# Spectral layer's way back for two blocks at a time, and seven products for all gates of one-node LSTMs

## The chip, the cores and the metric

The kernel runs on one core of a Trainium2 chip. Its time is the device time of one execution in microseconds, as the median over runs. A core has TensorE (PE, with weight loads listed apart as PEld), VectorE (DVE), ScalarE (ACT), GpSimd (POOL) and SyncE (SP), which issues most DMAs. Each runs its own queue of instructions in order; semaphores tie them together.

## What is computed

The input x has 128 batch entries of 64 nodes with 256 features, in float32. Four layers with skip connections follow each other, each on h = relu(layernorm(x)). Layer 0 is a graph convolution with batch norms, layer 3 an attention over 512 edges. The change touches layers 1 and 2:

```python
# layer 1 (U: eigenvectors of the graph's Laplacian, 64 x 64)
agg = jnp.einsum('mn,bnd->bmd', U.T, features)
h = jax.nn.relu(agg @ W1 + b1)
out = h @ W2 + b2
return jnp.einsum('nm,bmd->bnd', U, out)            # the way back

# layer 2: two graph convolutions, then LSTMs over windows of p nodes
for p in range(1, MAX_SKIP + 1):                     # 1 to 4
    nw = Tv // p
    wins = h[:, :nw * p, :].reshape(Bv * nw, p, Hd)
    last = _lstm_last(Wih[p - 1], Whh[p - 1], bih[p - 1], bhh[p - 1], wins)
    idx = jnp.arange(nw) * p + (p - 1)
    h = h.at[:, idx, :].set(last.reshape(Bv, nw, Hd))

# one step of the LSTM; state and cell start at zero
i, f, gg, o = jnp.split(x_t @ Wih.T + h @ Whh.T + bias, 4, axis=-1)
c = sigmoid(f) * c + sigmoid(i) * tanh(gg)
h = sigmoid(o) * tanh(c)
```

For p = 1 a window is a single node: there is no earlier state, the forget gate drops out, and h = sigmoid(o) * tanh(sigmoid(i) * tanh(gg)) overwrites each node.

## The kernel before

**Layout.** The 128 x 64 rows are cut into NB = 16 blocks of 8 batch entries. `X0` to `X15` are SBUF tiles of 128 partitions x 1024 floats that hold x, block by block. While layer 2's LSTMs run, x is spilled to DRAM and the X tiles serve as scratch; the nodes' features lie transposed in `big`, four groups of 32 batch entries (`nodes(q)`), each with two halves of 256 features on 128 partitions.

**Layer 1** (`layer1`, line 2030) is software-pipelined in an order written out by hand. Round i does `first(i)` (W1 and relu: "ps<-a,w"), `back(i - 1)` (the way back: eight 64x64-tiled matmuls "ps<-y,BDUT", then two adds onto X[i - 1]), `mixed(i + 1)` (agg: "ps<-BDU,h"), `second(i)` (W2 and bias: "pt<-w,g", then two adds into y), `end0(i + 3)` (layer 0's last transposes: "pe") and the layer norm of block i + 2. PSUM has four banks "ps", two "pt" and two "pe". Within a round a scheduler may move instructions between engines' queues by its own estimate of durations; `nc.hold(marks)` ties each instruction of a round to come after the previous round's last one on its engine.

**The LSTMs** (`windows`, line 2268) go through p = 1 to 4. The nodes of one p are cut into chunks of up to 16 windows x 16 + 16 batch entries; chunks are done two at a time. A step of one chunk (`lstm`, line 2358) first writes differences of its inputs into a tile T ("ls_tx<-big", a subtraction of 512 and two of 256 columns). Then `gates` computes two gates at once by Strassen's scheme in Winograd's form: seven products of halves of the weights and of the batch in place of eight. One product is two matmuls of 256 columns, one for each gate. Weight sums (`weights`, "ls_s", or sums in X tiles) stand ready; sums of products run through Z and U on DVE; sigmoids and tanhs run on ACT, in place in a tile V of "ls_g":

```python
a = product(1, "a", True)
self.act(Z, a, AF.Copy)
o.add(Z, Z, product(6, "b", True))
o.add(U, Z, product(7, "f", True))
o.add(V[:, :, 1, 1], U, product(5, "d", True))
a = product(2, "a", False)          # then activations of V[:, :, 0, 0] from PSUM
o.add(V[:, :, 1, 0], Z, product(4, "f", False))
o.add(V[:, :, 0, 1], Z, product(3, "d", False))
```

"f" and "d" are PSUM banks used twice: product 4 adds onto what product 7 left there, product 3 onto product 5, and so each has to wait until DVE has read the first sum.

For p = 1 a chunk needs three gates: input and candidate together by the seven products, and the output gate alone, by four direct matmuls of 512 columns (the branch `if p == 1 and len(xs) == 1`). The cell's product (128x1024), and the last state (`last_state`, two halves of 512), are multiplied on DVE. There are 4 groups x 4 = 16 chunks, so eight pairs.

**Order.** `nc.ordered` is off here: the same scheduler arranges each engine's instructions by its estimates, and dependences and the reuse of buffers bound it. `weights(p)` loads p's weights by DMA when the second pair of chunks of p - 1 begins. For p = 1 and 3 they lie in X tiles (X4 to X7 for the input weights, X0 to X3 for the recurrent ones), for p = 2 and 4 in tiles of their own. As the differences, weight sums and Z and U sums share DVE's queue, one that waits holds up those behind it.

Of the kernel before, what the change touches and what calls it, by code (L numbers as in the profile page):

```python
# [8 lines left out]
F32 = mybir.dt.float32  # L9
I32 = mybir.dt.int32  # L10
AF = mybir.ActivationFunctionType
ALU = mybir.AluOpType
# [901 lines left out]
class Fast:  # L914
# [28 lines left out]
    def act(self, out, a, f, **kw):  # L943
        return self.nc.scalar.activation(out, a, f, **kw)
# [499 lines left out]
B, N, D = 128, 64, 256  # L1444
P = 128
NB = 16
TPB = 4
BT = 512
# [18 lines left out]
class Kernel:  # L1467
# [35 lines left out]
    def begin(self):  # L1503
        nc, o, io = self.nc, self.o, self.io
        self.ident = self.c("ident", P, P)
        make_identity(nc, self.ident)
        self.ones = self.c("ones", P, P)
        nc.vector.memset(self.ones[:], 1.0)
        self.A, self.AT = self.c("A", N, N), self.c("AT", N, N)
        nc.sync.dma_start(self.A[:], io["adj"])  # L1510
        nc.sync.dma_start(self.AT[:], io["adj_t"])
        self.X = []
        for i in range(NB):
            self.X.append(self.c(f"X{i}", P, TPB, D))
        self.load_x(0)

    def load_x(self, i):
# [512 lines left out]
    def layer1(self, pool, psum, ps2, ps0, tables, after):  # L2030
        nc, o = self.nc, self.o
        (W1, W2), b1, b2 = self.W1, self.b1, self.b2
        nc.fresh()
        nc.ordered = True
        p = psum.tile([P, BT], F32, name="ps")
        self.warm(p[:, 0:P], 8)
        hs, as_, gs, ys = {}, {}, {}, {}

        def mixed(i):
            a = as_[i] = pool.tile([P, 2, BT], F32, name="a")  # L2040
            self.mix(psum, hs.pop(i), self.BDU, lambda dc, p: self.act_copy(a[:, dc, :], p[:]), True)

        def first(i):
            p = psum.tile([P, BT], F32, name="ps")
            a = as_.pop(i)
            for kc in range(2):
                self.mm(p[:], W1[:, kc, :], a[:, kc, :], kc == 0, kc == 1)
            g = gs[i] = pool.tile([P, BT], F32, name="g")
            self.act(g[:], p[:], AF.Relu, bias=b1[:, 0:1])

        def second(i):

            g = gs.pop(i)
            y = ys[i] = pool.tile([P, 2, 2, D], F32, name="y")
            for k in range(2):
                p = ps2.tile([P, 2, D], F32, name="pt")
                for c in range(2):
                    self.mm(p[:, c, :], g[:, (2 * k + c) * P:(2 * k + c + 1) * P], W2[:, 0, :])
                o.add(y[:, k, :, :], p[:], b2[:, None, :].to_broadcast([P, 2, D]))

        def back(i):

            y = ys.pop(i)
            ps = [psum.tile([P, 2, D], F32, name="ps") for r in range(2)]
            for c in range(2):
                for r in range(2):
                    s = slice(64 * r, 64 * r + 64)
                    self.mm(ps[r][64 * c:64 * c + 64], self.BDUT[s, s], y[s, :, c, :])
            for r in range(2):
                x = self.X[i][:].rearrange("p (k r) d -> p r k d", r=2)[:, r]  # L2070
                o.add(x, x, ps[r][:])


        self.features1(0)
        self.features1(1)
        self.residual(ps0, 0, (0, 2))
        by = self.moments(pool, 0)
        self.residual(ps0, 1, (0,))
        by = self.factors(pool, *by)
        self.residual(ps0, 1, (2,))  # L2080
        p = psum.tile([P, BT], F32, name="ps")
        self.warm(p[:, 0:P], 10)
        hs[0] = self.norm(pool, 0, by=by)
        by = self.moments(pool, 1)
        mixed(0)
        by = self.factors(pool, *by)
        hs[1] = self.norm(pool, 1, by=by)
        self.features1(2)
        marks = nc.mark()
        for i in range(NB + 1):  # L2090
            if i < NB:
                first(i)
            if i == 4:
                tables()
            if i:
                back(i - 1)
            if i + 1 < NB:
                mixed(i + 1)
            if i < NB:
                second(i)  # L2100
            if not i:
                self.residual(ps0, 2, (0, 2))
            if i + 3 < NB:
                self.end0(i + 3, ps0)
            if i + 2 < NB:
                hs[i + 2] = self.norm(pool, i + 2)

            nc.ordered = False
            nc.hold(marks)
            marks = nc.mark()  # L2110
            if i == NB - 1:
                nc.hold()
                after()
# [154 lines left out]
    def windows(self):  # L2268
# [4 lines left out]
        nc, o, io = self.nc, self.o, self.io  # L2273
        cx, (w, wq, gp, tp, zp, psum, pst) = self.stage([("lsw", 1), ("lswq", 1), ("lsg", 2), ("lst", 2), ("lsz", 2),
                                                         ("lsps", 7), ("lstps", 1)], "tile")
        with cx:
# [3 lines left out]
                nc.sync.dma_start(bias[:], io["L2_gnn_bih"].rearrange("q (k p) -> p q k", p=P))  # L2280
                nc.sync.dma_start(bh[:], io["L2_gnn_bhh"].rearrange("q (k p) -> p q k", p=P))
            o.add(bias[:], bias[:], bh[:])
            flat = [x[:].rearrange("p t d -> p (t d)") for x in self.X]
            self.c_, self.h_, self.th_ = Ring(flat[12:15]), Ring(flat[8:10]), Ring(flat[10:12])
            self.u_ = Ring([flat[15][:, 0:512], flat[15][:, 512:1024]])
            self.lp = gp, tp, zp, psum, bias
# [9 lines left out]
            def weights(p):  # L2296

                out = []
                for n, m in enumerate(("Wih", "Whh") if p > 1 else ("Wih",)):
                    t = load(None, n, None if p % 2 == 0 else 4 - 4 * n)  # L2300
                    ap = io[f"L2_gnn_{m}_t"][p - 1]
                    for kc in range(2):
                        nc.sync.dma_start(t[kc], ap[kc * P:(kc + 1) * P, :])
                    A = [[t[kc].rearrange("p (x k m) -> p x k m", k=2, m=P)[:, :, k, :] for kc in range(2)]
                         for k in range(2)]
                    S1, S2, S4 = (y.rearrange("p (x m) -> p x m", m=P) for y in t[2:5])
                    o.add(S1, A[1][0], A[1][1])
                    o.sub(S2, S1, A[0][0])
                    o.sub(S4, A[0][1], S2)
                    S3 = t[5].rearrange("p (x m) -> p x m", m=P) if len(t) > 5 else A[1][0]  # L2310
                    o.sub(S3, A[0][0], A[1][0])
                    out.append({1: A[0][0], 2: A[0][1], 3: S4, 4: A[1][1], 5: S1, 6: S2, 7: S3,
                                "A": A})
                return out

            ready = weights(1)
            for p in range(1, 5):
                Ws = ready
                nw = N // p
                parts = -(-nw // 16)  # L2320
                chunks = []
                for q in range(NG):
                    w0 = 0
                    for k in range(parts):
                        w1 = w0 + (nw - w0) // (parts - k)
                        chunks.append((q, w0, w1))
                        w0 = w1
                for n in range(0, len(chunks), 2):
                    if n == 2 and p < 4:
                        ready = weights(p + 1)  # L2330
                    if n == 2 and p == 4:
                        self.fetch(0, 8)
                        for i in range(8):
                            self.back(i, pst, "pt")
                    two = [dict(q=q, w0=w0, w1=w1) for q, w0, w1 in chunks[n:n + 2]]
                    two[-1]["last"] = p == 4 and n + 2 >= len(chunks)
                    for t in range(p):
                        for ch in two:
                            self.lstm(p, t, ch, Ws)
# [18 lines left out]
    def lstm(self, p, t, ch, Ws):  # L2358
# [25 lines left out]

        def gates(xs, fs):
            G = gp.tile([P, 2, 1024], F32, name="ls_g")
            if p == 1 and len(xs) == 1:
                for k in range(2):
                    ps = psum.tile([P, BT], F32, name="ps")
                    for kc in range(2):  # L2390
                        self.mm(ps[:, 0:2 * W].rearrange("p (w b) -> p w b", b=32), Ws[0]["A"][k][kc][:, xs[0], :],
                                node(kc), kc == 0, kc == 1)
                    self.act(G[:, 0, 2 * W * k:2 * W * (k + 1)].rearrange("p (h w b) -> p h w b", h=2, b=16),
                             ps[:, 0:2 * W].rearrange("p (w h b) -> p h w b", h=2, b=16), fs[0],
                             bias=bias[:, p - 1, 2 * xs[0] + k:2 * xs[0] + k + 1])
                return G
            n = len(xs)
            V = G[:, 0:n, 0:4 * W].rearrange("p x (k h w) -> p x k h w", k=2, h=2)
            banks = {}
# [57 lines left out]
        else:  # L2457
            self.last_state(H, at, W, s(G, 0), s(G, 1))

    def last_state(self, H, at, W, *factors):  # L2460

        for k in range(2):
            y = H[:, k, at, :].rearrange("p w (h b) -> p h w b", h=2)
            self.o.mul(y, *(x[:, 2 * W * k:2 * W * (k + 1)].rearrange("p (h w b) -> p h w b", h=2, b=16) for x in factors))

# [470 lines left out]
```

## Time and profile before

| | us |
|---|---|
| median of three runs | 2251.39 (2249.25 to 2252.05) |
| profiled execution | 2249.32 |
| its span | 2247.5 |
| PE busy | 2207.4 (98%) |
| DVE busy | 1629.2 (72%) |
| ACT busy | 1153.4 (51%) |
| POOL busy | 37.9 (2%) |
| LSTMs over single nodes, 672.19 to 825.34 | 153.15 |

The granted TensorE clock is 0.997 of full speed. Nearly all instructions are recorded at one helper's line, L800, so the profile's groups are told apart by engine, operation and tiles: "ps<-ls_tx,X" is a matmul into a PSUM tile ps, with ls_tx and X as its operands, and "x12" a run of twelve records. A matmul of full float32 leaves two records. Times are in us unless marked ns; a row's first number in the timeline is its start from the span's beginning, the second its duration up to the last record's end. In a group's row the numbers after the bar are the busy time, the mean of one in ns, and the idle time ahead of them with what ended it.

### The profile page before, as it was taken

To read this page: it belongs to the slowest core of one execution; us is meant where nothing else is said; L and a number is where in the kernel's file an instruction comes from. 1 tells how busy PE (TensorE), PEld (TensorE's weight loads), DVE (VectorE), ACT (ScalarE), POOL (GpSimd) and SP (SyncE) were. 2 spreads that over 40 slices of the span, in tenths; PEclk is the share of its full clock that TensorE was granted. 3 is DMA by queue.
4 is the path that set the end of the run, shared out by engine and by line. 5 is a ranking of instruction groups with operands and counts; after the bars stand their busy time and mean duration, and the time that the engine had idled before them with its cause. 6 is when DMAs were issued, how large, how long until landed. Compare 5 with 4: busy or idle time off the path is not lost.

```text
span 2247.5 us, 33965 instructions
## 1 busy us (share of the span) xinstructions
PE 2207.4 (98%) x12683; PEld 1627.7 (72%) x12683; DVE 1629.2 (72%) x4132; ACT 1153.4 (51%) x2522; POOL 37.9 (2%) x66
## 2 busy tenths in 40 slices
PE   7999998999999999999999999999999999999999
PEld 4554445667987778888999999888888655555654
DVE  8877576888658776676766676656955787777767
ACT  5667865665545663444444444434634664444431
POOL 1000000000220000000000000000000000000000
PEclk9999999999999999999999999999999999999999
DMA  6000210121010000000100002000001000000001
GB/s 181 1 1 17 69 57 23 66 76 30 1 57 1 1 19 1 1 1 1 39 1 1 1 1 70 7 1 1 13 1 55 26 1 15 17 18 20 15 25 48
DMA packets 61071, 54.89 MB, mean 24 GB/s; under 512 B 15203, under 2 KB 58724, under 8 KB 60900
## 3 DMA queue, kind: packets, MB, share of 16 engines
q1 hardware_dynamic: 60900, 52.66, 7.5%
q8 instruction: 101, 1.65, 0.3%
q14 instruction: 70, 0.57, 0.1%
HBM read 35.86 MB, written 16.78 MB: 23 GB/s over the span
## 4 chain that ended last, share of the span: by engine, by line
PE 77%; DVE 5%; ACT 1%; issue 1%; DMA 0%; DVEq 0%; ACTq 0%; SPq 0%
PE ps L800 69%; PE pt L800 4%; PE acc L800 3%; PE pe L800 1%; DVE sm_m L800 1%; DVE X L800 1%; DVE aw L800 1%; DVE XV L800 0%; ACT ls_g L800 0%; ACT h L800 0%; DVE lin_s L800 0%; DVE ls_s L800 0%; DVE lin_p L800 0%; DMA ed_a<-in_L_gnn_a_dram 0%; DVE hT L800 0%
## 5 line engine op out<-in xcount | busy, mean ns | idle before, releaser
L800 ACT ACTIVATE ls_g<-ls_g,ls_b 128x512 f32<-128x512 f32 (+4 forms) x472 | 243.3, 565 | 147.7 <-DVE ls_g L800 145.7
L800 ACT ACTIVATE ls_g<-ps,ls_b 128x256 f32<-128x256 f32 (+3 forms) x268 | 115.4, 470 | 335.4 <-PE ps L800 331.9
L800 PE MATMUL ps<-z,w 128*128 128x512 f32 x512 | 255.5, 621 | 0.0
L800 PE MATMUL ps<-big,X 128*128 128x176 f32 (+3 forms) x848 | 212.9, 367 | 0.1
L800 DVE TENSOR_TENSOR ls_g<-ls_z,ps 128x512 f32<-128x512 f32 (+5 forms) x258 | 147.4, 577 | 90.3 <-PE ps L800 88.6
L800 PE MATMUL ps<-ls_tx,X 128*128 128x160 f32 (+2 forms) x960 | 207.0, 327 | 1.6 <-DVE ls_tx L800 0.9
L800 PE MATMUL ps<-X,X 128*128 128x160 f32 (+2 forms) x918 | 205.8, 308 | 0.0
L800 PE MATMUL ps<-X,ls_w 128*128 128x256 f32 x640 | 190.6, 379 | 0.1
L800 PEld LDWEIGHTS ps<-ls_tx,X 128*128 128x128 f32 x960 | 161.8, 190 | 16.4 <-DVE X L800 4.8
L800 DVE TENSOR_TENSOR aw<-at,ed_OST 128x1024 f32<-128x1024 f32 x128 | 150.3, 1220 | 28.7 <-PE ps L800 28.5
L800 PEld LDWEIGHTS ps<-big,X 128*128 128x128 f32 x848 | 146.1, 190 | 29.6 <-issue 19.1
L800 ACT ACTIVATE r<-ps 128x512 f32<-128x512 f32 x256 | 129.3, 625 | 74.4 <-PE ps L800 74.3
L800 DVE TENSOR_TENSOR X<-ls_g 128x1024 f32<-128x1024 f32 (+2 forms) x108 | 117.5, 1088 | 50.6 <-ACT ls_g L800 50.6
L800 PEld LDWEIGHTS ps<-X,X 128*128 128x128 f32 x918 | 152.8, 190 | 0.6
L800 PE MATMUL ps<-X,ls_s 128*128 128x256 f32 x480 | 142.8, 379 | 0.0
L800 PEld LDWEIGHTS ps<-z,w 128*128 128x128 f32 x512 | 87.0, 190 | 66.6 <-issue 59.5
L800 PE MATMUL ps<-ls_tx,ls_s 128*128 128x256 f32 x464 | 134.9, 380 | 0.0
L800 PEld LDWEIGHTS ps<-X,ls_w 128*128 128x128 f32 x640 | 121.5, 190 | 16.6 <-DVE X L800 0.5
L800 PE MATMUL ps<-ls_tx,ls_w 128*128 128x256 f32 x464 | 133.4, 380 | 0.0
L800 PE MATMUL ps<-big,ls_w 128*128 128x256 f32 x464 | 132.0, 380 | 0.7 <-ACT ls_z L800 0.7
L800 PE MATMUL ps<-ed_S,Q 64*128 64x512 f32 x512 | 121.0, 604 | 0.9 <-DVE X L800 0.9
L800 PE MATMUL ps<-aw,ed_ODT 128*32 128x512 f32 x1024 | 121.7, 593 | 0.1
(575 smaller groups left out, 4010.4 us busy)
## 6 DMA issues: line engine op xcount, KB each, us to landing
X<-in_x_dram SPq DMA_DIRECT2D x32, 512.0 KB
xs<-X SPq DMA_DIRECT2D x16, 512.0 KB
X<-xs SPq DMA_DIRECT2D x16, 512.0 KB
out_dram<-X SPq DMA_DIRECT2D x31, 256.0 KB
X<-in_L_gnn_Wih_t_dram SPq DMA_DIRECT2D x4, 512.0 KB
ls_w<-in_L_gnn_Wih_t_dram SPq DMA_DIRECT2D x4, 512.0 KB
ls_w<-in_L_gnn_Whh_t_dram SPq DMA_DIRECT2D x4, 512.0 KB
w<-in_L_gnn_W_t_dram SPq DMA_DIRECT2D x2, 512.0 KB
```

Of the source, the lines that this page charges most:

```text
L800: i = method(*a, **kw)
```

## The change

In layer 1, `back` takes two blocks: after every even round's `first` it does blocks i - 2 and i - 1, all eight matmuls of one and then of the other, and then the four adds. The even block's results use the "ps" banks, the odd block's the "pt" banks.

For p = 1 the LSTMs go through a new function, `single`, for a pair of chunks at a time. It computes the differences of both chunks into a ring of three X tiles, input and candidate gates of the one chunk and of the other by seven products each as before, and then the output gates of *both chunks* by seven products in which the two matmuls of a product belong to the two chunks. The tile V comes from a ring of four pairs of X tiles. The last activations, of V[:, :, 0, 1], the cell's product with its tanh, and the last states are put off into a list `late`, which the next call empties just after its copy of product 1 (`nc.hold` puts them behind that copy on ACT). The cell's product runs on POOL, the last states on POOL too, but for the last pair's, which stay on DVE. X tiles are allocated in pairs (`X2`).

```diff
-        self.X = []
-        for i in range(NB):
-            self.X.append(self.c(f"X{i}", P, TPB, D))
+        self.X2 = [self.c(f"X{i}", P, 2, TPB, D) for i in range(0, NB, 2)]
+        self.X = [x[:, i] for x in self.X2 for i in range(2)]
...
-        def back(i):
-
-            y = ys.pop(i)
-            ps = [psum.tile([P, 2, D], F32, name="ps") for r in range(2)]
-            for c in range(2):
+        def back(*blocks):
+
+            parts = []
+            for i in blocks:
+                y, (banks, name) = ys.pop(i), ((psum, "ps"), (ps2, "pt"))[i % 2]
+                ps = [banks.tile([P, 2, D], F32, name=name) for r in range(2)]
+                for c in range(2):
+                    for r in range(2):
+                        s = slice(64 * r, 64 * r + 64)
+                        self.mm(ps[r][64 * c:64 * c + 64], self.BDUT[s, s], y[s, :, c, :])
+                parts.append((i, ps))
+            for i, ps in parts:
                 for r in range(2):
-                    s = slice(64 * r, 64 * r + 64)
-                    self.mm(ps[r][64 * c:64 * c + 64], self.BDUT[s, s], y[s, :, c, :])
-            for r in range(2):
-                x = self.X[i][:].rearrange("p (k r) d -> p r k d", r=2)[:, r]
-                o.add(x, x, ps[r][:])
+                    x = self.X[i][:].rearrange("p (k r) d -> p r k d", r=2)[:, r]
+                    o.add(x, x, ps[r][:])
 
...
-            if i:
-                back(i - 1)
+            if i and i % 2 == 0:
+                back(i - 2, i - 1)
...
-            flat = [x[:].rearrange("p t d -> p (t d)") for x in self.X]
+            flat = [x.rearrange("p t d -> p (t d)") for x in self.X]
+            self.late = []
+            self.g_ = Ring([self.X2[i][:].rearrange("p x t d -> p x (t d)") for i in (4, 5, 6, 0)])
+            self.t_ = Ring([flat[i] for i in (2, 3, 14)])
...
-                    out.append({1: A[0][0], 2: A[0][1], 3: S4, 4: A[1][1], 5: S1, 6: S2, 7: S3,
-                                "A": A})
+                    out.append({1: A[0][0], 2: A[0][1], 3: S4, 4: A[1][1], 5: S1, 6: S2, 7: S3})
...
+                    if p == 1:
+                        self.single(two, Ws[0], n + 2 >= len(chunks))
+                        continue
...
-            if p == 1 and len(xs) == 1:
-                for k in range(2):
-                    ps = psum.tile([P, BT], F32, name="ps")
-                    for kc in range(2):
-                        self.mm(ps[:, 0:2 * W].rearrange("p (w b) -> p w b", b=32), Ws[0]["A"][k][kc][:, xs[0], :],
-                                node(kc), kc == 0, kc == 1)
-                    self.act(G[:, 0, 2 * W * k:2 * W * (k + 1)].rearrange("p (h w b) -> p h w b", h=2, b=16),
-                             ps[:, 0:2 * W].rearrange("p (w h b) -> p h w b", h=2, b=16), fs[0],
-                             bias=bias[:, p - 1, 2 * xs[0] + k:2 * xs[0] + k + 1])
-                return G
...
 
-    def last_state(self, H, at, W, *factors):
+    def single(self, two, A, last):
+
+
+        nc, o = self.nc, self.o
+        _, _, zp, psum, bias = self.lp
+        I, F, G, O = range(4)
+        data = []
+        for ch in two:
+            H, at = self.nodes(ch["q"]), slice(ch["w0"], ch["w1"])
+            T = self.t_.next().rearrange("p (n w b) -> p n w b", n=4, b=16)
+            o.sub(T[:, 0:2], H[:, :, at, 16:32], H[:, 0, at, :].rearrange("p w (h b) -> p h w b", h=2))
+            o.sub(T[:, 2], H[:, 1, at, 16:32], T[:, 0])
+            o.sub(T[:, 3], H[:, 1, at, 0:16], T[:, 2])
+            data.append({1: H[:, 0, at, 0:16], 2: H[:, 1, at, 0:16], 3: H[:, 1, at, 16:32],
+                         5: T[:, 0], 7: T[:, 1], 6: T[:, 2], 4: T[:, 3]})
+
+        def gates(pairs, act):
+
+            tile = self.g_.next()
+            V = tile.rearrange("p x (k h w) -> p x k h w", k=2, h=2)
+            banks = {}
+
+            def product(m, bank, first):
+                if first:
+                    banks[bank] = psum.tile([P, 2, 256], F32, name="ps")
+                for i, (x, b) in enumerate(pairs):
+                    nc.tensor.matmul(banks[bank][:, i, :].rearrange("p (w b) -> p w b", b=16), A[m][:, x, :], b[m],
+                                     start=first and i == 0, stop=i == 1, skip_group_check=True)
+                return banks[bank][:]
+
+            Z = zp.tile([P, 2, 256], F32, name="ls_z")[:]
+            U = self.u_.next().rearrange("p (x w) -> p x w", x=2)
+            a = product(1, "a", True)
+            self.act(Z, a, AF.Copy)
+            nc.hold((None, None, nc.mark()[2]))
+            while self.late:
+                self.late.pop(0)()
+            nc.hold()
+            o.add(Z, Z, product(6, "b", True))
+            o.add(U, Z, product(7, "f", True))
+            o.add(V[:, :, 1, 1], U, product(5, "d", True))
+            a = product(2, "a", False)
+            act(V[:, :, 0, 0], a, 0)
+            o.add(V[:, :, 1, 0], Z, product(4, "f", False))
+            act(V[:, :, 1], V[:, :, 1], 1)
+            o.add(V[:, :, 0, 1], Z, product(3, "d", False))
+            self.late.append(lambda: act(V[:, :, 0, 1], V[:, :, 0, 1], 0))
+            return tile
+
+        def apart(out, a, k):
+            for i, (x, f) in enumerate(((I, AF.Sigmoid), (G, AF.Tanh))):
+                self.act(out[:, i], a[:, i], f, bias=bias[:, 0, 2 * x + k:2 * x + k + 1])
+
+        def together(out, a, k):
+            self.act(out, a, AF.Sigmoid, bias=bias[:, 0, 2 * O + k:2 * O + k + 1])
+
+        def cell(V):
+
+            def product():
+                nc.gpsimd.tensor_tensor(V[:, 0], V[:, 0], V[:, 1], op=ALU.mult)
+                soon.append(lambda: self.act(V[:, 1], V[:, 0], AF.Tanh))
+
+            self.late.append(product)
+
+        cells, soon = [], []
+        for b in data:
+            V = gates(((I, b), (G, b)), apart)
+            self.late += soon
+            soon.clear()
+            cell(V)
+            cells.append(V)
+        V = gates([(O, b) for b in data], together)
+        self.late += soon
+        for i, ch in enumerate(two):
+            self.late.append(lambda i=i, ch=ch: self.last_state(
+                self.nodes(ch["q"]), slice(ch["w0"], ch["w1"]), 256, V[:, i], cells[i][:, 1],
+                engine=None if last else nc.gpsimd))
+        if last:
+            while self.late:
+                self.late.pop(0)()
+
+    def last_state(self, H, at, W, *factors, engine=None):
 
         for k in range(2):
             y = H[:, k, at, :].rearrange("p w (h b) -> p h w b", h=2)
-            self.o.mul(y, *(x[:, 2 * W * k:2 * W * (k + 1)].rearrange("p (h w b) -> p h w b", h=2, b=16) for x in factors))
+            (engine or self.nc.vector).tensor_tensor(y, *(x[:, 2 * W * k:2 * W * (k + 1)].rearrange("p (h w b) -> p h w b", h=2, b=16) for x in factors), op=ALU.mult)
```

## The prediction

> **What bounds the kernel now.** I read the page first, its busy line and its chain of work that ended last, then the stage that changes most in the timeline.
>
> ```profile
> PE 2207.4 (98%) x12683; PEld 1627.7 (72%) x12683; DVE 1629.2 (72%) x4132; ACT 1153.4 (51%) x2522; POOL 37.9 (2%) x66
> PE 77%; DVE 5%; ACT 1%; issue 1%; DMA 0%; DVEq 0%; ACTq 0%; SPq 0%
> ```
>
> TensorE is the bound nearly everywhere, and GpSimd (POOL) is empty. So time falls only with fewer or shorter matmuls, and any new wait that reaches TensorE's queue is paid in full. The profiled execution took 2249.3 us, 1.8 us of it outside its span of 2247.5 us; the median of the runs is 2251.4. I make the sum against 2249.3 and quote it against the median. About 0.2%, 4.5 us, can be told from no change.
>
> The LSTMs over single nodes run from 672.19 to 825.34. The windows view says whether they leave TensorE any room, the timeline what one chunk takes:
>
> ```profile
> 672.19:825.34 153.15, 152.16 (x578) 109.40 (x577) 118.24 (x187) 93.24 (x161) 0.00 (x0) 1.00 0.01 4
> 797.78 2.75 PE L800 MATMUL ps<-ls_tx,X 128*128 128x256 f32 x12
> 807.25 2.75 PE L800 MATMUL ps<-ls_tx,X 128*128 128x256 f32 x12
> ```
>
> The columns of the first are the window, its length, busy time of PE, weight loads, VectorE (DVE), ScalarE (ACT) and POOL. PE is busy for 152.2 of 153.2 us. A chunk starts every 9.47 us, and 16 chunks make 151.5.
>
> **The seven products.** Starts of consecutive groups put a 256-column matmul at 0.431 us and a 512-column one at 0.862. Today a chunk has 14 of the short (input and candidate gates) and 4 of the long (the direct output gate): 14 × 0.431 + 4 × 0.862 = 9.48, which is the period. Afterwards a pair of chunks has three gate calls of 14 short ones: 42 × 0.431 = 18.1 against 18.95. That is −0.86 a pair, **−6.9 us** for eight pairs, if PE stays fed.
>
> **What feeds it.** In a call the products run in the order 1, 6, 7, 5, 2, 4, 3, each 2 × 0.431 = 0.862. With 0 at the first, they end at 0.86, 1.72, 2.59, 3.45, 4.31, 5.17, 6.03. Product 3 adds onto the bank that DVE has emptied with U + product 5, so this add must end before 5.17. I take DVE at 0.60 from start to start for 512 columns, ACT at 0.42 for 256 and 0.66 for 512 columns, 0.58 for the copy, 0.27 from a product to DVE, 0.03 from DVE to ACT (all from the stage's rows). Of the call before the output gates, product 4 ends at −0.86; its add runs −0.59 to 0.01, its two sigmoids and tanhs to 1.36, then ACT copies product 1 until 1.94 and applies the two held activations until 2.80. POOL can begin the cell's product at 2.87. DVE adds Z at 1.97 to 2.57 and U at 2.86 to 3.46; next in its order is a subtraction of two SBUF inputs (X differences of the chunk after next, 128x512, written early because its buffer in the ring of three is just free), and only then U + product 5.
>
> The cell's product of 128x1024 isn't in the trace on POOL. The nearest rows are layer 2's subtractions:
>
> ```profile
> L2168 POOL TENSOR_TENSOR X<-a,X 128x256 f32<-128x256 f32 x22 | 16.8, 763 | 1.7
> L2168 POOL TENSOR_TENSOR X<-a 128x512 f32<-128x512 f32 x11 | 13.9, 1267 | 264.6 <-ACT a L800 264.6
> ```
>
> 0.504 us for 256 more columns makes 1.267 + 512 × 1.97 ns = 2.28 us (1.27 at least, twice that at most); the last state's halves of 512 cost 1.27 each. DVE paid 1.22 and 0.65. All this is 2 × 2.28 + 4 × 1.27 = 9.6 us of POOL a pair of 18.1, so it keeps up. It does not run freely beside DVE, though:
>
> ```profile
> 559.08 2.32 POOL L2168 TENSOR_TENSOR X<-a,X 128x256 f32<-128x256 f32 x2
> 559.47 0.68 DVE L800 TENSOR_TENSOR y<-pt,w_b 128x512 f32<-128x512 f32 x1
> 560.74 0.68 DVE L800 TENSOR_TENSOR n_r<-n_r,n_v 128x4 f32<-128x4 f32 x1
> 579.12 1.53 POOL L2168 TENSOR_TENSOR X<-a,X 128x256 f32<-128x256 f32 x2
> 580.10 0.58 DVE L800 TENSOR_TENSOR n_r<-n_r,n_y 128x4 f32<-128x4 f32 x1
> 580.71 0.18 DVE L800 RECIPROCAL n_r<-n_r 128x4 f32<-128x4 f32 x1
> ```
>
> The tiny 128x4 product takes 0.16 elsewhere and 0.58 where POOL's pair ends at 580.65; the one at 560.74 ends with POOL's at 561.40. POOL's pair at 559.08 in turn takes 2.32 instead of 1.53, because DVE had the 512 subtraction at 560.16. DVE's add with a PSUM operand at 559.47 takes its ordinary 0.68 in the midst of POOL's work. So an operation of DVE with two SBUF inputs and one of POOL exclude each other for the whole instruction, and adds from PSUM go free.
>
> "Perfetto Trace Analysis" of the Trainium skill (Optimizing Scalar/DVE Operations) speaks against this move: DVE and GpSimd share a read port, so offloading between them might not help. Read without the restriction to two SBUF inputs, it would hold back Z, U and the two adds behind each POOL operation as well, an estimated (2.28 − 0.65) + 4 × (1.27 − 0.65), some 4 us more a pair; the row at 559.47 speaks against that reading, and I don't use it.
>
> So in the output-gate call the subtraction finds POOL busy from 2.87 to 5.15, runs to 5.75, U + product 5 follows until 6.35, and product 3 starts at 6.41 instead of 5.17: **+1.24 a pair**. Seven pairs write such a subtraction: **+8.7 us**. The product's price decides it: at 1.27 the stall is 0.2, at 4.5 it is 3.5 (0 and 24 us in all as ends); I take 1.24, by the extrapolation. The output gates' weights don't change, and their sigmoids merge to one instruction a tile, off the path.
>
> **POOL's last states.** They are 4 × 1.27 in the first call of the next pair, behind the copy, the held sigmoids (0.67) and the tanh (1.06), so from about 2.4 to 7.5. Twice, in pairs 1 and 2, the planned DVE order holds the two-node LSTMs' differences (reading these states, so waiting on POOL's last) ahead of Z + product 4. The subtraction then ends at 8.15, its 256 successor at 8.5, the add at 9.1, the activations at 10.4, the copy at 11.0, and product 2 of the next call begins at 11.05 instead of 9.48: +1.6, and more (3.3) where POOL came late itself. I take **+2 each, +4**. Nothing covers this; today DVE writes these states itself with no wait.
>
> **Into two-node windows.** In the last call DVE's order has a weight sum that waits for a DMA into X4, ahead of Z + product 4. The transfer starts only when the last output-gate call has read that buffer's slot. Today it is issued at 824.68 and the sum runs at 830.24, 5.5 us later, late by only 0.37; after the change the gate's add, its sigmoid, the copy and the last states queue behind it. From product 1 of that call, 0.86 + 5.6 = 6.5 against 5.44 is +1, and DVE's four last states (0.64 each) in front of the next Z add make 1.2 more: **+2.3** (0 to 4).
>
> **The start.** Today PE has 0.86 and 0.96 us of idle there, since differences are written at 672.39; they move ahead of 670. With the four weight sums at 667 to 671 leaving for a stage in which DVE has room: **−1.2** (−1.8 to +1).
>
> **Layer 1.** A block takes 7.32 us, PE bound:
>
> ```profile
> 456.62 1.88 PE L800 MATMUL ps<-a,w 128*128 128x512 f32 x4
> 458.43 1.09 PE L800 MATMUL ps<-y,BDUT 64*64 64x512 f32 x8
> 459.45 2.05 PE L800 MATMUL ps<-BDU,h 128*128 128x128 f32 x16
> 461.34 1.89 PE L800 MATMUL pt<-w,g 128*128 128x256 f32 x8
> ```
>
> Starts are 1.81 (from 456.62 to 458.43), 1.02, 1.89 and 1.72 apart. At the LSTMs' pace, 0.431 for 512 columns of one record and 0.108 for 128, the first and third should be 1.72, and the second 0.86 with its four 64x64 quarters side by side. The visit to 64-row matmuls thus costs 0.09 + 0.16 + 0.17, some 0.41. Two blocks adjoining pay it once: −0.41 in six pairs (the first two are split by other work), −2.5. Against it, X's adds come four at a time (2.4 us instead of 1.2), and the odd block's banks are now those of the second linear layer's output (pt), held until the fourth add; where that arrives 0.4 late nothing is left, at 0.6 it is a loss. I take **0** (−2.5 to +3).
>
> "TensorEngine Tiling (Array Packing)" (Key Properties) says that a change of tiling mode drains TensorE, without a price; alone it would make the layer the −2.5.
>
> **Sum:** −6.9 + 8.7 + 4 + 2.3 − 1.2 + 0 = +6.9, so 2256.2 on the profile and about **2258** against the median.
>
> **The rivals.**
> *Faster: POOL comes second.* The cell's product beats the subtraction by only 3.46 − 2.87 = 0.59 us. If ACT is that much later (a longer copy, a wait in its queue), DVE goes first and nothing of the 8.7 is paid. With layer 1's saving whole and the other waits at their low ends: −6.9 − 1.2 − 2.5 + 3.2 + 1 = −6.4, about 2245. For it: 0.59 is one ACT operation. Against: the same lateness would delay the Z add, and so the subtraction too. Chance 0.27.
> *Near nothing:* the same order, with the other terms as taken: −6.9 + 4 + 2.3 − 1.2 = −1.8, 2249.6. Chance 0.16.
> *The forecast:* 0.57, from +3 to +15.
> That the products aren't saved can't be: the matmul count is fixed by the code.
>
> **How the numbers follow.** The range leaves out the far ends: 2243 takes in the faster rival, 2267 a POOL product dearer by a third of a microsecond (2.3), 3.3 at each state wait (2.6), the DMA's wait at its end (1.7) and a start that brings little (2.4). Faster is 0.27 plus 0.02 of the middle case; same is 0.12 of the middle and 0.05 of the forecast's low end; the rest is slower.
>
> **What would show it.** Right: pairs of 19.3 us in the stage, PE idle in front of ps products with "<-DVE" as releaser once a pair, a 128x512 subtraction of DVE of about 2.3 us that ends with POOL's 128x1024. Wrong: pairs of 18.1, POOL's product starting after that subtraction, or a POOL product near 1.3 us; layer 1's pair off 14.65 by more than 0.3.

## The result, and the profile after

The changed kernel takes 2257.5 us (median of 8 runs, 2254.54 to 2260.13) against 2251.3 for the kernel before in the same measurement (2246.45 to 2252.34). The ratio is 1.0031, 95% interval 1.0022 to 1.0040: slower by 5 to 9 us, as forecast (2258). The profiled execution of the changed kernel has a span of 2257.9, 10.4 longer than that of before. The busy line and the chain of its page:

```profile
PE 2206.5 (98%) x12779; PEld 1646.8 (73%) x12779; DVE 1633.4 (72%) x4128; ACT 1155.3 (51%) x2522; POOL 112.6 (5%) x110
PE 73%; DVE 7%; issue 2%; ACT 1%; POOL 0%; DMA 0%; POOLq 0%; DVEq 0%; ACTq 0%; SPq 0%
```

TensorE's share of the chain fell from 77% to 73%, and DVE's rose from 5% to 7%: a hint to look for waits on DVE, no more, since 4% of the span is 90 us and the change some 10. The shares of busy time hardly tell it.

Three anchors on TensorE show where the 10.4 us arose. Layer 1's first agg (ps<-BDU,h) starts at 382.60 instead of 380.45, layer 2's first ps<-BDA,y of the steady part at 565.80 instead of 561.99, and the first product of the two-node LSTMs at 835.27 instead of 825.34.

- 2.15 us lie ahead of everything that the change touches. In the profiles of this study that anchor stands between 378.44 and 383.60 with no edit before it, so this is the spread between executions, which the medians average out.
- Layer 1: 3.81 − 2.15 = **+1.66**.
- The one-node LSTMs with their start: 9.93 − 3.81 = **+6.12**.
- What follows: **+0.5**.

So the change costs 8.3 us in the traces, inside the interval of the runs.

The stage in windows (window, length, busy PE, PEld, DVE, ACT, POOL) and steady pairs in the timeline of TensorE:

```profile
672.19:835.00 162.81, 151.60 (x696) 129.58 (x695) 120.13 (x177) 94.12 (x160) 74.18 (x44) 1.00 0.03 10
738.70 1.99 PE L800 MATMUL ps<-big,X 128*128 128x256 f32 x8 [1.02 <-DVE X L800]
758.06 1.99 PE L800 MATMUL ps<-big,X 128*128 128x256 f32 x8 [0.97 <-DVE X L800]
777.43 1.99 PE L800 MATMUL ps<-big,X 128*128 128x256 f32 x8 [0.98 <-DVE X L800]
```

A pair takes 19.36 us (758.06 − 738.70), against 18.10 for its 42 matmuls at 0.431 and 18.95 before. The 1.26 that is lost sits at one place, product 3 of the output-gate call, and is waited for from DVE. The engines around it:

```profile
753.53 0.90 ACT L800 ACTIVATE X<-X,ls_b 128x256 f32<-128x256 f32 x2
753.75 0.69 DVE L800 TENSOR_TENSOR ls_z<-ls_z,ps 128x512 f32<-128x512 f32 x1 [1.04 <-PE ps L800]
754.50 2.36 POOL L2517 TENSOR_TENSOR X<-X 128x1024 f32<-128x1024 f32 x1 [3.28 <-DVE ls_z L800]
754.54 0.69 DVE L800 TENSOR_TENSOR X<-ls_z,ps 128x512 f32<-128x512 f32 x1
755.15 2.26 DVE L800 TENSOR_TENSOR X<-big 128x512 f32<-128x512 f32 x1
756.07 1.03 PE L800 MATMUL ps<-X,X 128*128 128x256 f32 x4
757.33 0.68 DVE L800 TENSOR_TENSOR X<-X,ps 128x512 f32<-128x512 f32 x1
758.06 1.99 PE L800 MATMUL ps<-big,X 128*128 128x256 f32 x8 [0.97 <-DVE X L800]
```

Read it downwards. The held activations end at 754.43, POOL starts the cell's product at 754.50. U (X<-ls_z,ps) has a PSUM operand and runs beside it in its ordinary 0.69. The subtraction from `big` is recorded from 755.15 with 2.26 us instead of 0.69: it ends at 757.41, 0.55 after POOL's 756.86, about the 0.60 from start to start that such an operation takes when nothing holds it. Only then does U + product 5 run (X<-X,ps), and product 3 starts behind it, 1.13 late: the group ahead of it starts at 756.07 and its four records take 0.86. (Lateness, and the waits that are added up below, are counted like this, from start to start; the idle time in brackets, 0.97 here, counts from the modelled end of the matmul before and is shorter.) The group of eight records then lasts 1.99 instead of the 1.89 of one without a wait: 0.1 more for starting again, 1.23 of the 1.26.

POOL's groups give the durations that were extrapolated:

```profile
L2517 POOL TENSOR_TENSOR X<-X 128x1024 f32<-128x1024 f32 x16 | 37.9, 2366 | 68.7 <-ACT X L800 35.5 <-DVE ls_z L800 33.2
L2543 POOL TENSOR_TENSOR big<-X,X 128x512 f32<-128x512 f32 x28 | 36.3, 1328 | 26.6 <-ACT X L800 26.6
```

2.37 for the cell's product (2.28 taken) and 1.33 for half a last state (1.27).

The wait for POOL's last states, in pair 2, in the timeline of POOL, DVE and TensorE:

```profile
720.07 5.23 POOL L2543 TENSOR_TENSOR big<-X,X 128x512 f32<-128x512 f32 x4 [4.00 <-ACT X L800]
725.33 0.69 DVE L800 TENSOR_TENSOR ls_tx<-big 128x512 f32<-128x512 f32 x1 [2.61 <-POOL big L2543]
728.98 1.13 PE L800 MATMUL ps<-big,X 128*128 128x256 f32 x4 [1.08 <-ACT ls_z L800]
730.50 1.13 PE L800 MATMUL ps<-X,X 128*128 128x256 f32 x4 [0.39 <-DVE X L800]
```

DVE stands idle for 2.61 with Z + product 4 queued behind the two-node differences; ACT's copy is late for it, and TensorE waits 1.08 and 0.39 by the brackets, 1.24 and 0.66 from start to start.

### The profile page after: what moved, and what is told of

The parts are those of the page before. It is cut to its first block, busy times and chain, and to the rows that moved or that the text cites. A ratio compares the mean times of both kernels' runs of the same rounds, so it can differ in the third digit from the quotient of the medians.

```text
span 2257.9 us, 34205 instructions
## 1 busy us (share of the span) xinstructions
PE 2206.5 (98%) x12779; PEld 1646.8 (73%) x12779; DVE 1633.4 (72%) x4128; ACT 1155.3 (51%) x2522; POOL 112.6 (5%) x110
## 4 chain that ended last, share of the span: by engine, by line
PE 73%; DVE 7%; issue 2%; ACT 1%; POOL 0%; DMA 0%; POOLq 0%; DVEq 0%; ACTq 0%; SPq 0%
PE ps L800 65%; PE pt L800 4%; PE acc L800 3%; DVE X L800 2%; PE pe L800 1%; DVE sm_m L800 1%; DVE aw L800 1%; DVE n_st L800 1%; POOL big L2543 0%; ACT X L800 0%; DVE XV L800 0%; ACT ls_g L800 0%; DVE n_r L800 0%; DVE ls_z L800 0%; DVE y L800 0%
## 5 line engine op out<-in xcount | busy, mean ns | idle before, releaser
L800 PE MATMUL ps<-X,X 128*128 128x160 f32 (+2 forms) x1302 | 296.7, 329 | 3.8 <-DVE X L800 3.8
L800 ACT ACTIVATE ls_g<-ls_g,ls_b 128x512 f32<-128x512 f32 (+5 forms) x408 | 207.9, 559 | 126.4 <-DVE ls_g L800 124.1
L800 PEld LDWEIGHTS ps<-X,X 128*128 128x128 f32 x1302 | 225.3, 190 | 15.7 <-DVE X L800 5.4
L800 ACT ACTIVATE ls_g<-ps,ls_b 128x256 f32<-128x256 f32 (+2 forms) x204 | 80.5, 438 | 303.6 <-PE ps L800 302.2
L800 PE MATMUL ps<-big,X 128*128 128x256 f32 (+2 forms) x816 | 182.1, 334 | 7.5 <-DVE X L800 5.9
L800 DVE TENSOR_TENSOR ls_g<-ls_z,ps 128x512 f32<-128x512 f32 (+3 forms) x226 | 125.5, 561 | 76.0 <-PE ps L800 74.1
L800 PEld LDWEIGHTS ps<-big,X 128*128 128x128 f32 x816 | 139.1, 190 | 18.8 <-DVE X L800 8.4
L800 PE MATMUL ps<-ls_tx,X 128*128 128x160 f32 (+1 forms) x704 | 146.3, 307 | 0.6 <-ACT ls_g L800 0.6
L800 DVE TENSOR_TENSOR X<-ls_z,ps 128x512 f32<-128x512 f32 (+4 forms) x185 | 112.7, 610 | 41.8 <-PE ps L800 37.9
L800 DVE TENSOR_TENSOR X<-ls_g 128x1024 f32<-128x1024 f32 (+2 forms) x92 | 97.9, 1064 | 39.0 <-ACT ls_g L800 38.9
```

Source lines behind the costliest of these rows:

```text
L800: i = method(*a, **kw)
```

## The experiments

All times are medians with the kernel before run on the same chip; "ratio" is to that kernel. Where the runs overlap, the trace's own intervals decide.

**Each part alone.** The first has before's LSTMs and the new `back`, the second the new LSTMs and before's `back`.

> The kernel before with layer 1's two-block way back alone. The traces put layer 1 at +1.7 us after the change: steady pairs of blocks at 14.86 instead of 14.65, with PE idle 0.31 for DVE's adds onto X ahead of pt<-w,g. Theory: this is the change's own doing, so about 1.5 us slower than before (0.5 to 3), pairs of 14.86. Rival: halved mode switches save 2.5 us and the 1.7 are a start that varies from run to run; then 2 us faster and pairs below 14.6.

> The changed one-node LSTMs with layer 1 as before. Theory: the whole rest of the loss is here, +5 us against before (3 to 7), steady pairs of chunks at 19.36 as in the changed kernel, layer 1 at 14.65 a pair of blocks. Rival: the stage's order was spoilt by what layer 1 left behind on DVE; then pairs near 18.1 and a time below before's.

`back` alone: 2249.9 us against 2250.8, ratio 1.0002 (0.9992 to 1.0011), which can't tell 1.5 from nothing. Its trace can:

```profile
450.51 1.09 PE L800 MATMUL ps<-y,BDUT 64*64 64x512 f32 x8
452.38 2.05 PE L800 MATMUL ps<-BDU,h 128*128 128x128 f32 x16
454.74 1.99 PE L800 MATMUL pt<-w,g 128*128 128x256 f32 x8 [0.30 <-DVE X L800]
465.36 1.09 PE L800 MATMUL ps<-y,BDUT 64*64 64x512 f32 x8
```

Pairs of blocks take 14.85 (450.51 to 465.36), with 0.30 of idle ahead of every second pt<-w,g. The rival's "below 14.6" is out. LSTMs alone: 2258.3, ratio 1.0036 (1.0024 to 1.0048); blocks at 14.65 a pair, the stage 159.53 us long against 159.56 in the changed kernel, with the same waits. The two parts don't touch each other; three quarters of the loss in the traces, 6.12 of 8.3, are the LSTMs'.

**The cell's product in two halves.** POOL then has a boundary at which DVE's subtraction can get its turn:

```diff
-nc.gpsimd.tensor_tensor(V[:, 0], V[:, 0], V[:, 1], op=ALU.mult)
+for s in (slice(0, 512), slice(512, 1024)):
+    nc.gpsimd.tensor_tensor(V[:, 0, s], V[:, 0, s], V[:, 1, s], op=ALU.mult)
```

> The changed kernel with the cell's product on POOL as two halves of 512 columns, all else alike. Theory (exclusion by whole instructions): the subtraction gets its turn between the halves, at about +4.2 of the call instead of +5.2, so the stall falls from 1.26 to 0.2 or 0.4 a pair, pairs of 18.3 to 18.5, 5 to 7 us less than the changed kernel, though POOL works longer (2 x 1.33 against 2.37). Rival (the two engines share a rate, or DVE waits until POOL's queue is empty): POOL's longer work makes it 0.3 a pair worse, pairs of 19.5 to 19.7, 2 us more than the changed kernel.

2249.5 us, ratio 0.9994 (0.9985 to 1.0003): 8 us less than the changed kernel, from one line that gives POOL more to do. The timeline of the same place:

```profile
747.87 2.51 POOL L2518 TENSOR_TENSOR X<-X 128x512 f32<-128x512 f32 x2 [3.49 <-ACT X L800]
749.13 0.69 DVE L800 TENSOR_TENSOR X<-ls_z,ps 128x512 f32<-128x512 f32 x1
749.74 1.19 DVE L800 TENSOR_TENSOR X<-big 128x512 f32<-128x512 f32 x1
750.85 0.67 DVE L800 TENSOR_TENSOR X<-X,ps 128x512 f32<-128x512 f32 x1
751.58 2.00 PE L800 MATMUL ps<-big,X 128*128 128x256 f32 x8
```

POOL's two halves end at 750.38 and DVE's subtraction 0.55 later, the add begins at 750.85, and TensorE's group is 0.1 late. From pair 3 on no wait longer than that is left. But the subtraction didn't go between the halves, as the theory had it: the second had begun, and it waited for that. And this edit changed two things: POOL began at 747.87, before ACT's held activations (748.12 to 749.01), where the whole product began after them. One of the halves holds none of the values that are activated late, so POOL could begin 1.26 us ahead of U (749.13), where the whole product began 0.04 ahead of it. The gain could come from the early start alone.

So another run cuts the product so that each part has a piece of every quarter, and depends on the held activations as the whole does:

```diff
-nc.gpsimd.tensor_tensor(V[:, 0], V[:, 0], V[:, 1], op=ALU.mult)
+i, f = (V[:, x].rearrange("p (n w) -> p n w", n=4) for x in range(2))
+for s in (slice(0, 128), slice(128, 256)):
+    nc.gpsimd.tensor_tensor(i[:, :, s], i[:, :, s], f[:, :, s], op=ALU.mult)
```

> The changed kernel with the cell's product on POOL in two instructions of 4 x 128 columns, each of which holds a part of every quarter and so depends on the held activations as the whole does. In the run with halves of 512, one half doesn't need them and began 1.26 us earlier; this one changes the length of the instruction alone. Theory (exclusion by whole instructions, the one that waits goes first at the boundary): the subtraction runs between the two, from about 4.2 to 4.8 of the call instead of 5.2 to 5.8, the stall falls from 1.26 to 0.2 or 0.3, pairs of 18.3 to 18.5 and 2251. Rival A: POOL's second instruction follows the first at once, so that the subtraction waits for both; pairs of 19.4 to 19.6, 2258. Rival B (it was the early start that helped): the same as rival A in time, but with the subtraction between the two and product 3 as late as before.

2251.6 us, ratio 1.0006 (0.9996 to 1.0016), pairs of 18.29 (751.35 to 769.64). Its timeline:

```profile
748.87 2.96 POOL L2519 TENSOR_TENSOR X<-X 128x512 f32<-128x512 f32 x2 [3.49 <-DVE ls_z L800]
748.90 0.69 DVE L800 TENSOR_TENSOR X<-ls_z,ps 128x512 f32<-128x512 f32 x1
749.51 1.18 DVE L800 TENSOR_TENSOR X<-big 128x512 f32<-128x512 f32 x1
750.62 0.68 DVE L800 TENSOR_TENSOR X<-X,ps 128x512 f32<-128x512 f32 x1
751.35 1.99 PE L800 MATMUL ps<-big,X 128*128 128x256 f32 x8
```

POOL starts level with U, as in the changed kernel, and its pair now takes 2.96: DVE's subtraction ends at 750.69 in the midst of it. It waited for POOL's first part and went ahead of the second. POOL does more work and finishes later, and the stall is gone all the same. That settles the mechanism: exclusion by whole instructions, with the waiting engine next in turn. Both rivals of this run are out.

**The subtraction behind the add.** The odd chunk's differences are tied behind U + product 5 (`self.v11` is that add's mark):

```diff
+nc.hold((None, self.v11 if j else None, None))
 T = self.t_.next().rearrange("p (n w b) -> p n w b", n=4, b=16)
```

> The changed kernel, where DVE issues the odd chunks' differences behind U + product 5 of the output-gate call instead of ahead of it. Theory (whole-instruction exclusion of DVE's subtraction by POOL's product, in front of the add that product 3 needs): the stall of 1.26 a pair goes in six or seven pairs, steady pairs 18.1 to 18.3, 7 to 9 us less than the changed kernel, so about 2249.5. Rival A: the add itself is held up by POOL; pairs stay at 19.3. Rival B: the two subtractions now in front of Z + product 4 pass the wait on to the next call's copy; pairs of 18.6 to 19.3.

2256.2 us, ratio 1.0028 (1.0015 to 1.0040): not the 2249.5 of the theory. Product 3 no longer waits in that call, so rival A (the add itself held up) is out. But the pairs still take 19.20, with TensorE's wait now in the next call (DVE, POOL and TensorE in the timeline of this run):

```profile
756.55 2.17 DVE L800 TENSOR_TENSOR X<-big,X 128x256 f32<-128x256 f32 x3
757.01 5.29 POOL L2546 TENSOR_TENSOR big<-X,X 128x512 f32<-128x512 f32 x4 [3.06 <-ACT X L800]
758.64 0.68 DVE L800 TENSOR_TENSOR ls_z<-ls_z,ps 128x512 f32<-128x512 f32 x1
760.16 1.13 PE L800 MATMUL ps<-X,X 128*128 128x256 f32 x4 [0.81 <-DVE X L800]
```

Three small subtractions, which need some 1.1 to 1.3 together (four took 1.43 at 673.60 in the kernel before, two 0.88 at 760.39 in the changed one), now meet POOL's first last state instead of the cell's product and end 2.17 after they began. Z of the next call is late, and product 4 with it (0.81 idle). This is rival B in kind: the exclusion stays, and the queue only meets another POOL instruction.

**The two-node differences later.** They are tied behind pair 5.

```diff
+if p == 2 and not t:
+    self.nc.hold((None, self.done1[5], None))
 T = tp.tile([P, 4, 256], F32, name="ls_tx")...
```

> The changed kernel, where DVE issues the first differences of the two-node LSTMs (which read POOL's last states of pairs 0 and 1) behind pair 5 instead of inside pairs 1 and 2. Theory: the two waits for POOL's fourth last state go, in the trace 0.54 + 0.65 + 1.24 + 0.66 = 3.1 us of PE's idle, and nothing else; about 2254.4, the stalls of 1.1 to 1.2 a pair stay. Rival: the wait is POOL's own lateness and turns up at the next reader of a last state's or a cell's tile; no gain, 2257.5.

2258.8 us, ratio 1.0034 (1.0025 to 1.0044): no gain that the runs show. In the trace the waits in pairs 1 and 2 (3.1 us with their parts) are gone, and 1.73 came back in pair 6, where the same differences now meet the last states of that pair as two-SBUF operations. The stage is 1.36 shorter, not 3.1. Half of the rival held: not the same wait, but the same engine.

**The cell's product on DVE; the last states on DVE.** Each takes one kind of work back from POOL.

```diff
-nc.gpsimd.tensor_tensor(V[:, 0], V[:, 0], V[:, 1], op=ALU.mult)
+nc.vector.tensor_tensor(V[:, 0], V[:, 0], V[:, 1], op=ALU.mult)
```

> The changed kernel with the cells' products on DVE instead of POOL (last states stay on POOL). Theory: DVE's chain of Z, U and U + product 5 has only some 0.65 us to spare in a call, and the product of 1.13 lands between Z and U: product 4 then waits 0.3 in each of two calls, product 3 up to 0.7 in the output-gate call, where the subtraction is still ahead of its add; 0.6 to 1.3 a pair, so the time stays within 3 us of the changed kernel (2254 to 2260). Rival: the exclusion with POOL is the only cost; then pairs of 18.1 to 18.3 and 2249.

2254.9 us, ratio 1.0026 (1.0016 to 1.0036). With no such product on POOL, steady pairs are no shorter: 19.77 (754.68 to 774.45), with TensorE late by 0.59, 0.55 and 0.20 in each. The sum, 1.34, is near the theory's 0.6 to 1.3, but it hardly comes from DVE's chain. Most of it lies in the call in which POOL does the last states:

```profile
752.46 4.10 POOL L2543 TENSOR_TENSOR big<-X,X 128x512 f32<-128x512 f32 x3 [0.16 <-ACT X L800]
753.11 0.92 DVE L800 TENSOR_TENSOR X<-big,X 128x256 f32<-128x256 f32 x1
754.55 0.89 DVE L800 TENSOR_TENSOR X<-big,X 128x256 f32<-128x256 f32 x1
754.68 1.13 PE L800 MATMUL ps<-X,X 128*128 128x256 f32 x4 [0.43 <-DVE X L800]
756.09 1.99 PE L800 MATMUL ps<-big,X 128*128 128x256 f32 x8 [0.28 <-DVE X L800]
762.00 1.13 PE L800 MATMUL ps<-X,X 128*128 128x256 f32 x4
```

In this run's order small subtractions from `big` stand between DVE's sums of that call, and each takes some 0.9 beside POOL's last states instead of 0.42; products 4 and 3 (754.68 and 756.09) are late behind them. The two calls that hold the cell's product on DVE lose 0.20 (762.00) and nothing. So the rival's 18.1 to 18.3 didn't come, but the run does not show that DVE lacks the room: it moved the product and left the exclusion by the last states.

```diff
-engine=None if last else nc.gpsimd))
+engine=None))
```

> The changed kernel with all last states on DVE, cells' products on POOL. Theory: the two waits for POOL's fourth last state go (3.1 us), the stalls of 1.14 a pair by the cell's product stay, and DVE has 4 x 0.65 more a pair, most of it in the first call whose chain has 0.65 to spare: 0 to 1.5 a pair; 2255 to 2264. Rival: POOL's last states were what made DVE late; then all but the 1.14s go, 2252 or less.

2256.8 us, ratio 1.0029 (1.0020 to 1.0038). The two waits for last states are gone, the wait by the cell's product is 1.19 in each of pairs 1 to 6, and pairs take 19.55. Both runs keep a loss, each mostly by the work that stays on POOL. No run has both kinds of work on DVE, so whether that would have been faster stays open.

**Cures together.** First the halves, the later differences and before's `back`:

> Both cures and layer 1 as before: the cell's product in two halves on POOL, the two-node LSTMs' first differences behind pair 5, one block's way back at a time. Theory: the terms add: 2249.5 (the split alone) - 3.1 - 1.6 = 2244.8, ratio to before about 0.9973; the stage has stalls only in pair 0 (some 2.5 us). Rival: the terms overlap, and the time stays at 2248 to 2250.

2248.0 us, ratio 0.9991 (0.9981 to 1.0001). The stage takes 150.99 against 159.56, and 153.15 before. That is 3 us above the theory's 2244.8; 1.7 of them is what the later differences brought back in pair 6.

The same with the new `back`, the odd block's adds written first (`for i, ps in reversed(parts)`):

> The same two cures with layer 1's two-block way back, but X's adds of the odd block (whose results hold the pt banks) ahead of the even block's. Theory: the wait of 0.31 ahead of pt<-w,g goes, steady pairs of blocks fall from 14.86 to 14.5 or less, layer 1 gains 1 us on before instead of losing 1.6; about 2243.5. Rival: the even block's ps banks are now held longer and the wait moves to ps<-BDU,h or ps<-a,w; pairs stay at 14.8 and the time at 2246.

2248.5 us, ratio 0.9995 (0.9985 to 1.0004). The scheduler issued X<-X,ps ahead of X<-X,pt all the same, and the pairs stayed at 14.85. It says nothing on the theory.

Then two more edits: the cell's products of pair 0 on DVE, because the two-node weights' sums collide with POOL there (`ls_s` at 684.94 takes 2.71 in the changed kernel, and TensorE is idle for 1.64 ahead of 688.30), and the two-node differences behind the second gate call of pairs 4 and 5:

```diff
+if two[0]["q"] == 0 and two[0]["w0"] == 0:
+    o.mul(V[:, 0], V[:, 0], V[:, 1])           # else the two halves on POOL
+self.nc.hold((None, self.done1[5 if w0 else 4], None))
```

> One block's way back as before, the cell's product in halves on POOL but for pair 0, where it is on DVE (the two-node weights' sums collide with POOL there), and the two-node LSTMs' first differences held behind the second gate call of pairs 4 and 5, where POOL has neither last states nor a product to do. Theory: the 6.2 us of PE's idle that the run with both cures left (2.6 in pair 0, 1.7 in pair 6, the rest in a tenth a pair) fall to 2 or less, so the stage takes 146.5 to 147.5 and the time is 4 us lower than with both cures, 2244 (ratio to before 0.997 to 0.998). Rival: DVE in pair 0 and the moved differences stall as much where they now are; 2248.

2247.9 us, ratio 0.9986 (0.9976 to 0.9995): faster than before, by 1 to 5 us. The waits of pairs 0 and 1 fell from 2.6 to 1.1 together, with 0.45 more in pair 2. The moved differences cost 1.2 in each of pairs 4 and 5, so the stage takes 150.0, not 147.

Last, the same with the new `back` and the odd block's adds tied ahead of the even block's (`nc.vector.hold = nc.mark()[1]` between the two):

> The same with layer 1's two-block way back, and the odd block's adds onto X put ahead of the even block's on DVE by a tie (the run that only wrote them in that order left DVE's order as it was). Theory: pt<-w,g no longer waits 0.31, pairs of blocks fall from 14.86 to 14.5, layer 1 is 0.5 to 1.5 below before's, and the time 2 to 3 us below the run with back as before by the trace. Rival: the even block's ps banks, now held longer, make ps<-BDU,h or ps<-a,w wait; pairs of 14.7 to 14.9.

2244.6 us, ratio 0.9982 (0.9973 to 0.9991), the fastest of the study, though its interval overlaps that of the run before. Layer 1 in its timeline:

```profile
447.69 1.09 PE L800 MATMUL ps<-y,BDUT 64*64 64x512 f32 x8
448.60 1.04 PE L800 MATMUL pt<-y,BDUT 64*64 64x512 f32 x8
449.57 2.05 PE L800 MATMUL ps<-BDU,h 128*128 128x128 f32 x16
451.46 1.89 PE L800 MATMUL pt<-w,g 128*128 128x256 f32 x8
461.98 1.09 PE L800 MATMUL ps<-y,BDUT 64*64 64x512 f32 x8
```

A pair of blocks takes 14.29 against 14.65 before and 14.86 in the changed kernel, and pt<-w,g has no idle any more. From ps<-BDU,h to the first steady ps<-BDA,y it is 180.12, against 182.39 with `back` alone as changed and 180.75 in the run with `back` as before. (In these three profiles the layer's first group lasts 2.81; in those of before and of the changed kernel it lasts 3.60 and 3.64, and the same interval is 181.54 and 183.20. Only profiles with a like start can be compared.) The rival (ps banks late) is out.

## Why the prediction was right

It came within 1 us of the median, and its main mechanism is the one the runs show. That it came so close is partly luck: some of its smaller terms were off and cancelled.

- **The products, −6.9.** The count and the pace held: 19.36 less the 1.13 and 0.1 of the wait leaves 18.1 a pair.
- **The cell's product in front of the subtraction, +8.7.** Six waits at product 3, in pairs 1 to 6, of 1.13 to 1.20: 7.0 us. In pair 0 DVE's subtraction did go first (693.10, POOL's product at 693.54), as the faster rival had it, but the loss only moved: the small differences behind it were held in turn, by the product (one took 1.98 at 694.29) and then by the first last state (two took 1.97 at 698.33), and product 4 of pair 1's first call came 1.68 late. 8.6 in all, 9.3 with 0.1 for each new start. In the steady pairs the product, U and the subtraction lay as worked out. The product in two equal parts, begun at the same time, shows that it is this exclusion; the subtraction behind the add, the product on DVE and the last states on DVE show that order alone, or taking one kind of work off POOL, does not give the time back.
- **Layer 1, 0.** Mis-sized: the second linear layer did wait for the odd block's pt banks, as named, but longer than taken. From start to start it came 0.47 late (0.31 of idle), and 0.1 for the new start makes 0.57 a pair, more than what is saved: +1.66 with the split first pairs. With the adds in the other order the saving is there, 0.36 a pair where 0.41 was expected.
- **Last states, +4.** 0.54 + 0.65 in pair 1 and 1.24 + 0.66 in pair 2, 3.1, with new starts 3.5.
- **Into two-node windows, +2.3.** Mis-sized: 0.56. The weights' transfer was taken at before's 5.5 from issue to the sum; it took 3.7 (issued at 830.29, sum at 833.99; why it was shorter stays open), so the sum held DVE up for only 0.36, and the next product wasn't late for it. The last states on DVE (837.09 to 839.59), taken at 1.2, and a weight sum stand ahead of the product that is 0.56 late, at 841.44.
- **The start, −1.2.** TensorE has no idle there now, against the 1.5 us lost in before's stage (the 0.96 of the prediction is a row of the weight loads at 688.26, and their wait is for a sum, not for differences; the matmuls lost 1.1 at 674.08 and 0.4 there). But pair 0's second call lost 1.8 that I had not seen, by the same exclusion, where the sums of the two-node weights met POOL's first product.

The three errors (+1.7, −1.7 and +1.5 or so) and the rest make the traces' 8.3 against the 6.9 predicted; the medians moved by 6.2. The warning of the Trainium skill, "Perfetto Trace Analysis" (Optimizing Scalar/DVE Operations), that moving work between DVE and GpSimd might not help fits this result. Its reading without the restriction, in which DVE waits for POOL in every operation, would have added an estimated 4 us a pair; U's row beside POOL at 754.54 speaks against that, as the row of before did. The rival by which the subtraction goes first came about in pair 0 alone; in the steady pairs POOL began 0.65 ahead of it, close to the 0.59 of the sum.

## What to carry to other kernels

Moving elementwise work to an idle GpSimd is not free while VectorE stands at a tight chain: look for VectorE instructions with two SBUF operands that are queued ahead of the chain, and charge each with what is left of GpSimd's running instruction. Shorter GpSimd instructions gave nearly all of it back here; a change of order alone only moved the wait to the next one, and so did taking half of the work back. In a kernel bound by TensorE, a buffer that is freed later (here two PSUM banks) can cost more than the saved work, and the order of the freeing operations decides it; tie it where a scheduler won't keep it.

## What the runs showed of the hardware

- Between two GpSimd instructions that stand ready, VectorE's waiting one goes first: its subtraction ran in the middle of a pair that took 2.96 for it, against some 2.5 for two halves without one between them.
- After each wait TensorE's first group took 0.1 us longer than its matmuls need (1.99 instead of 1.89 for eight records, 1.13 instead of 1.03 for four); at a stall a pair this is a twelfth of the 1.26 lost.
- The time until layer 1 begins differed by 5.2 us between profiled executions (378.44 to 383.60) with the same code ahead of it, so effects of 2 us were read from the traces' own intervals.
